# Gated update of a graph network: the new state moves from GpSimd and TensorE transposes to VectorE, and its rows go through DRAM

## Chip, cores and metric

The kernel runs on one core of a Trainium2 chip. The metric is the device time of one execution in microseconds (us); the median of several runs is given where there are several. Everything is computed in float32.

## The reference, cut to what matters

There are 128 graphs of 128 nodes with 256 channels. Layer 0 is a gated update (a GRU cell) over a normalized state `h`; its result is added to `x`. Layer 1 works on the first 25 nodes of each graph only and adds its result to these.

```python
h = jnp.maximum(_layernorm(x, axis=-1), 0.0)
...
xc = jnp.transpose(x, (0, 2, 1))
h = jax.nn.relu(_bn(_conv1d(xc, conv1_w, 0), ...))
h = _bn(_conv1d(h, conv2_w, 8), ...)
x_conv = jnp.transpose(jax.nn.relu(h + xc), (0, 2, 1))
...
x_nmp = jnp.einsum('bnm,bmd->bnd', A, msg)
x_in = jnp.concatenate([x_conv, x_nmp], axis=-1)
gi = x_in @ w_ih.T + b_ih
gh = x @ w_hh.T + b_hh
...
r = jax.nn.sigmoid(gi_r + gh_r)
z = jax.nn.sigmoid(gi_z + gh_z)
nn_ = jnp.tanh(gi_n + r * gh_n)
return (1.0 - z) * nn_ + z * x          # here x is h
...
x = x + _L0_gnn_ref(h, adj, ...)
h = jnp.maximum(_layernorm(x, axis=-1), 0.0)
x = x + _L1_gnn_ref(h, adj, ...)        # changes x[:, :25] only
```

## The kernel before

The work is tiled in 32 groups (`NQ`) of four graphs. It has three stretches. First come the normalization, the first convolution and a Fourier form of the second one (`stage_a`, `stage_b`), in two batches, with the neighbour sums (`early`) beside them; the states `hTd` and the neighbour sums `xmd` are kept in DRAM. Then comes the gated stage (its first new state is computed at 719.7 us), `stage_c(q)`, one group after the other, and beside it layer 1: `rows(q)` normalizes the 32 first rows of the four graphs of a group, `prepare(blk)` builds the adjacency of a block of 16 graphs (4 groups, 8 blocks), `block(blk)` runs its two graph convolutions. At the end stands what is left of layer 1.

The order of the instructions is written by a small planner (`Lane`, `Order`, L156 to L208): each of the functions above is a generator, and `yield a, b` tells the planner that the step took `a` us of TensorE and that its next step is due `b` us later at the earliest. The planner emits the steps of several lanes into one program per engine; each engine runs its own list in order. A `yield` is thus no wait on the chip: the waits come from the data (semaphores that the framework sets), and an instruction whose data is late holds up all that stands behind it on its engine.

In `stage_c` a group works on channels in the partitions and on 512 columns (4 graphs of 128 nodes). The names are `hT` (the state h, tile hTc in the profile, three buffers), `xm` (neighbour sums), `xc` (convolution), `r` (first the reset gate r, then the new state n), `z` (the update gate), `xt` (x, for the sum), each of the last three with one buffer. Products go through `part` (L754) into three PSUM banks named gat and five named tmp. `sums` (L597) makes the differences tc, th and tm on VectorE, tc at the start of a group and th, tm of the next group during it. The last step of a group (L874 to L911) is what is changed:

- ScalarE takes tanh of the two channel halves (L877).
- GpSimd computes, for each half, d = h - n (L880), d = d z (L881) and the new state d + n, written into z in another order of its columns (L883): six operations on 128x512 for each group.
- At least 11 us of planner time later, inside the next group, TensorE turns the result in eight 128x128 transposes (L900) into two tmp banks, so that nodes are in the partitions; VectorE adds x to it, for the first 32 nodes into `X1[blk]`, the tile of layer 1 (L903), for the others into xt (L904, L906).
- GpSimd's queue stores xt to the output in four DMAs (L909), with runs of 1 KB.
- x itself was loaded into xt by SP's queue in four DMAs (L381, called in L831), in rows of 1 KB, in the middle of the group. The tile z of the next group is taken only after these stores have been emitted (L821).

`rows(q)` starts once the group is in `C_DONE`: VectorE's bn_stats on 128x256 of `X1` (L958), aggregation, a power on GpSimd (L961), the scaling on VectorE (L964) and a relu on ScalarE (L965). `prepare` starts with four DMAs of adjacency entries in runs of 100 B (aj, L977), eight small sums on GpSimd (L983) and five reductions on VectorE (L988). `block` stores its rows through GpSimd's queue (L1120).

Of the kernel before, what the change touches and what calls it, by code (L numbers as in the profile page):

```python
# [9 lines left out]
FP = mybir.dt.float32  # L10
# [9 lines left out]
P = 128  # L20
# [187 lines left out]
def kernel(ctx: ExitStack, tc: tile.TileContext, x, adj, consts, vecs, w_se, conv1_w,  # L208
# [14 lines left out]
    wfd = dr.tile([F, D, D], FP, name="wfd")  # L223
    xmd = [dr.tile([P, 2, 512], FP, name=f"xmd{q}") for q in range(NQ)]
    yd = [dr.tile([P, F, D], FP, name=f"yd{b}") for b in range(NBAT)]


    cst = cp.tile([P, CONSTS.shape[1]], FP, name="cst")
# [150 lines left out]
    def load_x(t, q):  # L379
        for j in range(GB):  # L380
            nc.sync.dma_start(out=t[j * WIDE:(j + 1) * WIDE],  # L381
                              in_=x[q * GB + j].rearrange("(t n) c -> n t c", n=WIDE))
# [343 lines left out]
    def stage_c(q):  # L726
# [45 lines left out]


        xs = [(0, hT, None), (2, xm, None), (1, xc, None)]
        r = fr.tile([P, 2, 512], FP, tag="r", name=f"r{q}")
        u2 = fr.tile([P, 2, D], FP, tag="u2", name=f"u2{q}")
        u3 = fr.tile([P, 2, D], FP, tag="u3", name=f"u3{q}")
        r1, r2 = r[:, :, :D], r[:, :, D:]
        early = [(0, hT, th), (2, xm, tm)]
        p1, p6, p5 = bank(wrz, 0), bank(wrz, 5), bank(wrz, 4)  # L780
        part(p1, wrz, 0, xs, True, True)
# [2 lines left out]
        for operation in todo:  # L784
            operation()
        yield 2.6, 0.0
        for ps, i in ((p6, 5), (p5, 4)):
            part(ps, wrz, i, early, True, False)
            yield 1.75, 0.0
# [1 line left out]

        ve = fr.tile([P, 3, 1, D], FP, tag="ve", name=f"ve{q}")
        va, vb, vt = ve[:, 0], ve[:, 1], ve[:, 2]
        r11, r12, r21, r22 = r[:, 0:1, :D], r[:, 0:1, D:], r[:, 1:2, :D], r[:, 1:2, D:]

        def gate(dst, src, row):
            nc.vector.scalar_tensor_tensor(dst, src, v("b_hh", 4 + row), dst,
                                           op0=ALU.add, op1=ALU.mult)
# [4 lines left out]
        h6, h7 = product(wh, 5, xh, ptmp), product(wh, 6, xh, ptmp)  # L803
        nc.vector.tensor_tensor(va, va, h6, ALU.add)
        nc.vector.tensor_tensor(vb, va, h7, ALU.add)
        yield 1.3, 0.0
        part(p1, wrz, 1, xs, False, True, True)
        sigmoid(r1, p1, 0)
# [2 lines left out]
        nc.vector.tensor_tensor(u2, u2, p6, ALU.add)  # L811
        part(h1, wh, 1, xh, False, True, True)
        gate(r11, h1, 0)
        yield 1.3, 0.0
        part(p5, wrz, 4, xs[2:], False, True)
        some_sums(q + 1, 2)
        yield 0.87, 0.0
        if q + 1 in IN:
            convolved(q + 1, IN[q + 1][0])
            yield 1.8, 0.0  # L820
        while q and q - 1 not in C_DONE:  # L821
            yield 0.0, 0.5
        z = fr.tile([P, 2, 512], FP, tag="z", name=f"z{q}")
        z1, z2 = z[:, :, :D], z[:, :, D:]
        nc.vector.tensor_tensor(u3, u2, product(wrz, 6, xs), ALU.add)
        nc.vector.tensor_tensor(z2, u3, p5, ALU.add)
        sigmoid(z2, z2, 2)
        some_sums(q + 1, 2)
        yield 2.6, 0.0
        xt = fr.tile([P, 4, D], FP, tag="xt", name=f"xt{q}")  # L830
        load_x(xt, q)  # L831
        nc.vector.tensor_tensor(z1, u3, product(wrz, 3, xs), ALU.add)
        sigmoid(z1, z1, 2)
        nc.vector.tensor_tensor(vt, vb, product(wh, 3, xh, ptmp), ALU.add)
# [40 lines left out]
        nc.vector.tensor_tensor(r12, r12, p5, ALU.add)  # L875
        for dc in (1, 0):
            nc.scalar.activation(r[:, dc], r[:, dc], AF.Tanh, bias=v("b_ih", 4 + dc))  # L877

            d = hT[:, dc]
            nc.gpsimd.tensor_sub(d, d, r[:, dc])  # L880
            nc.gpsimd.tensor_mul(d, d, z[:, dc])  # L881
            pat = "p (j t n) -> p t j n"
            nc.gpsimd.tensor_add(z[:, dc].rearrange("p (t j n) -> p t j n", t=4, j=GB),  # L883
                                 d.rearrange(pat, j=GB, t=4),
                                 r[:, dc].rearrange(pat, j=GB, t=4))
        G_DONE.add(q)
        yield 0.87, 11.0


        blk = q // QS  # L890
        while blk > 2 and blk - 3 not in F_DONE:
            yield 0.0, 0.5
        if blk not in X1:
            X1[blk] = fr.tile([P, QS, D], FP, tag="x1", name=f"x1_{blk}", bufs=3)
        for h in range(2):
            po = ptmp.tile([P, 2, D], FP, tag="tmp", name=f"po{q}_{h}")
            for i in range(2):
                t = 2 * h + i
                for dc in (1, 0):
                    nc.tensor.transpose(po[:, i, dc * P:(dc + 1) * P],  # L900
                                        z[:, dc, t * P:(t + 1) * P], ident)
            if h == 0:
                nc.vector.tensor_add(X1[blk][:, q % QS], xt[:, 0], po[:, 0])  # L903
                nc.vector.tensor_add(xt[:, 1], xt[:, 1], po[:, 1])  # L904
            else:
                nc.vector.tensor_add(xt[:, 2:], xt[:, 2:], po)  # L906
        yield 0.9, 1.5
        for j in range(GB):
            nc.gpsimd.dma_start(out=out[q * GB + j, WIDE:].rearrange("(t n) c -> n t c", n=WIDE),  # L909
                                in_=xt[j * WIDE:(j + 1) * WIDE, 1:4])  # L910
        C_DONE.add(q)  # L911


# [55 lines left out]
    def prepare(blk):  # L969

        while not (blk - 1 in P_DONE and blk - 2 in {-2, *B1_DONE}):
            yield 0.0, 1.0
        pool, pool2, b1 = S["pool"], S["pool2"], S["b1"]
        ac, r4 = S["ac"][blk % 2], S["r4"][blk % 2]
        aj = pool.tile([NN, SB, NN], FP, tag="dd", name=f"aj{blk}")
        for i in range(GB):
            nc.sync.dma_start(out=aj[:, i % 2 * 2 + i // 2::GB],  # L977
                              in_=adj[blk * SB + i:(blk + 1) * SB:GB, :NN, :NN]
                              .rearrange("b n m -> n b m"))
        yield 0.0, 4.0  # L980

        for r, n, w in _runs():
            nc.gpsimd.tensor_tensor(b1[:, :, r:r + w], aj[:, :, n:n + w],  # L983
                                    ident[:NN, None, n:n + w].to_broadcast([NN, SB, w]),
                                    ALU.add)
        dg = pool2.tile([NN, SB, NG], FP, tag="dg", name=f"dg{blk}")
        for g in range(NG):
            nc.vector.reduce_sum(dg[:, :, g], b1[:, :, OFFS[g]:OFFS[g] + SIZES[g]],  # L988
                                 axis=mybir.AxisListType.X)
        yield 0.0, 7.0  # L990

        pa = ptmp.tile([P, SB // 2, RP], FP, tag="tmp", name=f"pa{blk}")
        for p in range(SB // 2):
            nc.tensor.matmul(pa[:, p], b1[:, 2 * p:2 * p + 2, :].rearrange("n s r -> n (s r)"),
                             c("et")[:NN, :RP], start=True, stop=True)
        nc.vector.tensor_mul(ac, pa, c("same")[:, None, :].to_broadcast([P, SB // 2, RP]))

        pdg = ptmp.tile([P, SB // 2, 2, NG], FP, tag="tmp", name=f"pdg{blk}")
        nc.tensor.matmul(pdg.rearrange("p a s g -> p (a s g)"), c("et")[:NN],
                         dg.rearrange("n b g -> n (b g)"), start=True, stop=True)  # L1000
        dsel = pool.tile([P, SB // 2, 2 * NG], FP, tag="dsel", name=f"dsel{blk}")
        nc.vector.tensor_mul(dsel, pdg.rearrange("p a s g -> p a (s g)"),
                             c("sgrp")[:, None, :].to_broadcast([P, SB // 2, 2 * NG]))
        dm = pool.tile([P, SB // 2], FP, tag="dm", name=f"dm{blk}")
        zo = pool.tile([P, SB // 2], FP, tag="zo", name=f"zo{blk}")
        nc.vector.reduce_sum(dm, dsel, axis=mybir.AxisListType.X)
        nc.vector.tensor_scalar(zo, dm, 0.0, None, op0=ALU.is_equal)
        nc.vector.tensor_add(dm, zo, dm)
        nc.gpsimd.tensor_tensor(dm, dm, c("mhalf"), ALU.pow)
        nc.gpsimd.tensor_mul(zo, zo, dm)  # L1010
        nc.gpsimd.tensor_sub(dm, dm, zo)
        yield 2.0, 7.0

        dd = pool.tile([P, SB // 2, RP], FP, tag="dd", name=f"dd{blk}")
        nc.vector.tensor_mul(dd, c("diag")[:, None, :].to_broadcast([P, SB // 2, RP]),
                             dm[:, :, None].to_broadcast([P, SB // 2, RP]))
        nc.vector.tensor_mul(ac, ac, dm[:, :, None].to_broadcast([P, SB // 2, RP]))
        yield 0.0, 6.0
        pg = ptmp.tile([P, SB // 2, RP], FP, tag="tmp", name=f"pg{blk}")
        nc.tensor.matmul(pg, c("ones2"), dd, start=True, stop=True)  # L1020
        nc.vector.tensor_mul(ac, ac, pg)
        yield 0.9, 3.0

        pr4 = ptmp.tile([P, QS, 2, RP], FP, tag="tmp", name=f"pr4{blk}")
        nc.tensor.matmul(pr4.rearrange("p q a r -> p (q a) r"), c("e4"), ac,
                         start=True, stop=True)
        for j in range(GB):
            s = slice(j * WIDE, (j + 1) * WIDE)
            nc.vector.tensor_copy(r4[s, :, j % 2 * 2 + j // 2, :], pr4[s, :, j % 2, :NR])
        yield 0.9, 1.0  # L1030
        P_DONE.add(blk)
# [112 lines left out]
    for bat, (during_a, during_b) in enumerate(((0.66, 0.5), (0.2, 0.65))):  # L1144
        if bat:
# [13 lines left out]
    groups = Lane([stage_c(q) for q in range(NQ)], ahead=2)  # L1159
    second = [setup_1()] + [part(blk) for blk in range(NBLK) for part in (prepare, block)]  # L1160
    beside.weight = 0.5
    order.run(loads, groups, beside, Lane([rows(q) for q in range(NQ)], ahead=2),
              Lane(second, ahead=2, weight=0.2))


# [39 lines left out]
```

## Time and profile before

| what | value |
|---|---|
| time, median of 3 runs | 2028.95 us (2023.29 to 2034.73) |
| profiled execution, its time | 2029.67 us |
| profiled execution, its span | 2027.9 us |
| mean TensorE clock granted | 0.996 |
| TensorE busy | 1989.1 us, 98% |
| VectorE busy | 1285.4 us, 63% |
| GpSimd busy | 742.3 us, 37% |
| ScalarE busy | 683.7 us, 34% |
| DMA packets | 190266, 281.91 MB |
| GpSimd's short DMA issues of xt (L909) | 128, 569 ns each |

The profile is of one execution. The span goes from the first to the last instruction; the execution's time holds 1.8 us more. PE is TensorE, PEld its weight loads, DVE VectorE, ACT ScalarE, POOL GpSimd and SP the engine that only issues DMAs. A row of a group shows line, engine, operation, tiles (output <- inputs), shapes and count, then busy time and mean duration, then the idle time of the engine just before these instructions and what ended it. The chain that ended last is followed back from the last instruction, at each step to what released it. The issue of a DMA is an instruction on its queue's engine; the duration of the issue is not the time of the transfer.

### The profile page before, as it was taken

The numbers are of one execution on the slowest core, as the hardware profiler recorded it, in microseconds if no ns is written. First come the engines' busy times: TensorE is split into PE (matmuls) and PEld (weight loads), VectorE is DVE, ScalarE is ACT, GpSimd is POOL, SyncE is SP. The second block draws the span as 40 slices with busy tenths as digits, with TensorE's granted clock in tenths as the row PEclk, the third lists the DMA queues.
The fourth block names the chain that finished last, engine by engine and source line by source line (L and its number), as shares of the span: only waits on it lengthen the run. The fifth ranks groups of instructions, "written<-read, shape, count | busy, mean of one in ns | idle before, by whom it ended". The sixth has DMA issues, their size and how long they took to land.

```text
span 2027.9 us, 34053 instructions
## 1 busy us (share of the span) xinstructions
PE 1989.1 (98%) x12852; PEld 1651.6 (81%) x12852; DVE 1285.4 (63%) x2807; ACT 683.7 (34%) x1547; POOL 742.3 (37%) x898
## 2 busy tenths in 40 slices
PE   7998999999999999999999999999999999999998
PEld 5667888889888888878788888878888888878875
DVE  6774445875433566766775775677577757766743
ACT  4663222444222344232322322232233322222233
POOL 3552666333656022622332233224323323332330
PEclk9999999999999999999999999999999999999999
DMA  9997879654887633432322322323232322232122
GB/s 215 296 279 229 275 253 287 209 163 156 265 264 240 191 109 89 149 93 74 95 73 84 104 74 73 104 79 84 79 105 68 90 86 92 81 98 84 37 82 53
DMA packets 190266, 281.91 MB, mean 139 GB/s; under 512 B 23745, under 2 KB 143494, under 8 KB 190102
## 3 DMA queue, kind: packets, MB, share of 16 engines
q1 hardware_dynamic: 157062, 185.46, 31.5%
q0 software_dynamic: 32656, 93.98, 14.2%
q8 instruction: 102, 1.67, 0.4%
q14 instruction: 62, 0.51, 0.1%
q10 hardware_dynamic: 384, 0.28, 0.1%
HBM read 187.34 MB, written 92.27 MB: 138 GB/s over the span
## 4 chain that ended last, share of the span: by engine, by line
PE 91%; DVE 3%; issue 2%; DMA 1%; POOL 1%; ACT 1%; SPq 0%; ACTq 0%; DVEq 0%; POOLq 0%
PE p L754 41%; PE pa L530 7%; PE pm L641 5%; PE ph L1062 5%; PE pz L1071 5%; PE pc L421 5%; PE pb L530 3%; PE pf L432 3%; PE pi L711 3%; PE px L667 3%; PE pw L476 2%; PE ph L410 1%; PE po L900 1%; PE py L1045 1%; PE pse L625 1%
## 5 line engine op out<-in xcount | busy, mean ns | idle before, releaser
L880 POOL TENSOR_TENSOR hTc<-hTc,r 128x512 f32<-128x512 f32 x64 | 88.5, 1383 | 255.5 <-ACT r L877 255.4
L530 PE MATMUL pa<-wf,X 128*128 128x256 f32 x640 | 152.2, 381 | 0.0
L562 DVE SCALAR_TENSOR_TENSOR y<-pa,kk 128x512 f32<-128x512 f32 x78 | 53.8, 690 | 151.3 <-ACT kk L561 151.3
L909 POOL DMA_DIRECT2D out<-xt x128 | 72.0, 569 | 175.3 <-DVE xt L906 172.2
L754 PE MATMUL p<-th,wrz 128*128 128x256 f32 x512 | 134.5, 385 | 0.0
L754 PE MATMUL p<-tc,wrz 128*128 128x256 f32 x512 | 131.5, 379 | 0.0
L754 PE MATMUL p<-tm,wrz 128*128 128x256 f32 x512 | 131.4, 379 | 0.0
L530 PEld LDWEIGHTS pa<-wf,X 128*128 128x128 f32 x640 | 118.1, 190 | 16.2 <-issue 2.0
L641 PE MATMUL pm<-wmsg,hT 128*128 128x256 f32 x512 | 123.6, 387 | 2.2 <-DMA wmsg<-in_w_msg 2.2
L421 PE MATMUL pc<-c1w,hTa 128*128 128x256 f32 x512 | 121.7, 384 | 1.2 <-ACT hTa L412 1.2
L641 PEld LDWEIGHTS pm<-wmsg,hT 128*128 128x128 f32 x512 | 97.0, 193 | 18.4 <-ACT ef L629 2.6
L1064 ACT ACTIVATE hh<-ph,vec 128x96 f32<-128x96 f32 (+3 forms) x160 | 63.8, 401 | 140.7 <-PE ph L1062 131.6
L1062 PE MATMUL ph<-yz,w 128*128 128x96 f32 (+3 forms) x640 | 109.7, 325 | 1.0 <-issue 1.0
L754 PEld LDWEIGHTS p<-th,wrz 128*128 128x128 f32 x512 | 94.6, 190 | 19.2 <-issue 7.4
L421 PEld LDWEIGHTS pc<-c1w,hTa 128*128 128x128 f32 x512 | 94.4, 191 | 18.4 <-DVE h L424 4.8
L723 ACT ACTIVATE xc<-xc,t_bn 128x256 f32<-128x256 f32 x128 | 58.0, 500 | 149.1 <-DVE xc L720 149.1
L754 PEld LDWEIGHTS p<-tm,wrz 128*128 128x128 f32 x512 | 97.3, 190 | 13.2
L1071 PE MATMUL pz<-hh,w 128*128 128x96 f32 (+3 forms) x640 | 107.3, 321 | 0.0
L1062 PEld LDWEIGHTS ph<-yz,w 128*128 128x128 f32 x640 | 88.2, 193 | 21.3 <-issue 15.2
L754 PEld LDWEIGHTS p<-tc,wrz 128*128 128x128 f32 x512 | 94.9, 190 | 11.7
L1071 PEld LDWEIGHTS pz<-hh,w 128*128 128x128 f32 x640 | 86.6, 191 | 17.7
L754 PE MATMUL p<-hTc,wrz 128*128 128x256 f32 x384 | 98.9, 380 | 0.0
(200 smaller groups left out, 4580.1 us busy)
## 6 DMA issues: line engine op xcount, KB each, us to landing
wf<-wfd SPq DMA_DIRECT2D x160, 256.0 KB
wfd<-ws POOLq DMA_DIRECT2D x64, 320.0 KB, 9.5
yd<-y POOLq DMA_DIRECT2D x80, 256.0 KB, 4.2
yt<-yd SPq DMA_DIRECT2D x64, 320.0 KB
w<-in_W SPq DMA_DIRECT2D x40, 512.0 KB
xa<-in_x SPq DMA_DIRECT2D x128, 128.0 KB
hTd<-hTa POOLq DMA_DIRECT2D x32, 512.0 KB, 6.9
hT<-hTd SPq DMA_DIRECT2D x32, 512.0 KB
```

Of the source, the lines that this page charges most:

```text
L421: nc.tensor.matmul(pc[:, i], hT[:, k, (2 * h + i) * N:(2 * h + i + 1) * N], c1w[:, k], start=(k == 0), stop=(k == 1))
L432: nc.tensor.matmul(pf[:, i, :F * NB], h1[:, 2 * h + i, k * P:(k + 1) * P], fwd, start=True, stop=True)
L530: nc.tensor.matmul(ps, xk(k), WF[f][:, k, s], start=(k == 0), stop=(k == 1))
L641: nc.tensor.matmul(pm[:, i], hT[:, k, j * N:(j + 1) * N], LATE["wmsg"][:, k], start=(k == 0), stop=(k == 1))
L667: nc.tensor.matmul(px[:, dc, i], msgs[h][:, i, dc * P:(dc + 1) * P], aT[:, 2 * h + i], start=True, stop=True)
L711: nc.tensor.matmul(pi[w * WIDE:(w + 1) * WIDE, :, :, n].rearrange("p k g c -> p g k c"), inv[:F, o:o + WIDE], yt[:, n // 2::2].rearrange(" ...
L754: nc.tensor.matmul(ps[:, m], w[:, i, k, m * P:(m + 1) * P], factor(i, x, t), start=first and j == 0, stop=last and j == len(n) - 1, skip_g ...
L880: nc.gpsimd.tensor_sub(d, d, r[:, dc])
L909: nc.gpsimd.dma_start(out=out[q * GB + j, WIDE:].rearrange("(t n) c -> n t c", n=WIDE), in_=xt[j * WIDE:(j + 1) * WIDE, 1:4])
L1062: nc.tensor.matmul(ph, w1[:, k, m * P:(m + 1) * P], yz[:, k, :, o:o + n], start=(k == 0), stop=(k == 1))
L1064: nc.scalar.activation(hh[:, m], ph, AF.Relu, bias=v("b1", g * 4 + m))
L1071: nc.tensor.matmul(pz, w2[:, g, m, cc * P:(cc + 1) * P], hs[g][:, m], start=(m == 0), stop=(m == 3))
```

## The change

The new state is computed by VectorE instead of GpSimd, for one channel half at a time, at two places in the following group (`turned`): three 128x512 operations and one VectorE transpose, which turns blocks of 32x32 and writes into the group's hT. A third place (`returned`) adds the x of the group in one operation on 128x1024 and stores the sum to a new DRAM tensor `x1d[q]` in four DMAs of GpSimd's queue. The 32x32 blocks leave the result in an order in which 32 neighbouring channels of a node are together: xt has this order too, x is loaded into it in four DMAs of GpSimd's queue, and both the load and the store move runs of 32 floats (128 B), 1024 of them in each DMA. A new generator `fetch(q)`, in a lane of its own, is due 10 us of planner time after `returned`: it loads the first 32 nodes of the four graphs from `x1d[q]` to `X1` and copies the other 96 from DRAM to the output, both through GpSimd's queue; 9 us later the group counts as done for `rows`. TensorE's eight transposes, their PSUM banks, and the wait of the planner for the group before (L821) are gone. The tile r of a group is now taken after the second `turned`. For the last group the three steps follow one another at once. In `prepare` the small sums of GpSimd are due 13 us after their loads instead of 4, and the reductions 5 us after the sums.

```diff
@@ -223,6 +223,7 @@
     wfd = dr.tile([F, D, D], FP, name="wfd")
     xmd = [dr.tile([P, 2, 512], FP, name=f"xmd{q}") for q in range(NQ)]
     yd = [dr.tile([P, F, D], FP, name=f"yd{b}") for b in range(NBAT)]
+    x1d = [dr.tile([GB, N, D], FP, name=f"x1d{q}") for q in range(NQ)]
 
 
     cst = cp.tile([P, CONSTS.shape[1]], FP, name="cst")
@@ -772,10 +773,8 @@
 
 
         xs = [(0, hT, None), (2, xm, None), (1, xc, None)]
-        r = fr.tile([P, 2, 512], FP, tag="r", name=f"r{q}")
         u2 = fr.tile([P, 2, D], FP, tag="u2", name=f"u2{q}")
         u3 = fr.tile([P, 2, D], FP, tag="u3", name=f"u3{q}")
-        r1, r2 = r[:, :, :D], r[:, :, D:]
         early = [(0, hT, th), (2, xm, tm)]
         p1, p6, p5 = bank(wrz, 0), bank(wrz, 5), bank(wrz, 4)
         part(p1, wrz, 0, xs, True, True)
@@ -784,6 +783,7 @@
         for operation in todo:
             operation()
         yield 2.6, 0.0
+        turned(q - 1, 1)
         for ps, i in ((p6, 5), (p5, 4)):
             part(ps, wrz, i, early, True, False)
             yield 1.75, 0.0
@@ -791,7 +791,6 @@
 
         ve = fr.tile([P, 3, 1, D], FP, tag="ve", name=f"ve{q}")
         va, vb, vt = ve[:, 0], ve[:, 1], ve[:, 2]
-        r11, r12, r21, r22 = r[:, 0:1, :D], r[:, 0:1, D:], r[:, 1:2, :D], r[:, 1:2, D:]
 
         def gate(dst, src, row):
             nc.vector.scalar_tensor_tensor(dst, src, v("b_hh", 4 + row), dst,
@@ -803,6 +802,10 @@
         h6, h7 = product(wh, 5, xh, ptmp), product(wh, 6, xh, ptmp)
         nc.vector.tensor_tensor(va, va, h6, ALU.add)
         nc.vector.tensor_tensor(vb, va, h7, ALU.add)
+        turned(q - 1, 0)
+        r = fr.tile([P, 2, 512], FP, tag="r", name=f"r{q}")
+        r1, r2 = r[:, :, :D], r[:, :, D:]
+        r11, r12, r21, r22 = r[:, 0:1, :D], r[:, 0:1, D:], r[:, 1:2, :D], r[:, 1:2, D:]
         yield 1.3, 0.0
         part(p1, wrz, 1, xs, False, True, True)
         sigmoid(r1, p1, 0)
@@ -811,6 +814,7 @@
         nc.vector.tensor_tensor(u2, u2, p6, ALU.add)
         part(h1, wh, 1, xh, False, True, True)
         gate(r11, h1, 0)
+        returned(q - 1)
         yield 1.3, 0.0
         part(p5, wrz, 4, xs[2:], False, True)
         some_sums(q + 1, 2)
@@ -818,17 +822,18 @@
         if q + 1 in IN:
             convolved(q + 1, IN[q + 1][0])
             yield 1.8, 0.0
-        while q and q - 1 not in C_DONE:
-            yield 0.0, 0.5
         z = fr.tile([P, 2, 512], FP, tag="z", name=f"z{q}")
+        xt = fr.tile([P, 16, 2, WIDE], FP, tag="xt", name=f"xt{q}")
         z1, z2 = z[:, :, :D], z[:, :, D:]
         nc.vector.tensor_tensor(u3, u2, product(wrz, 6, xs), ALU.add)
         nc.vector.tensor_tensor(z2, u3, p5, ALU.add)
         sigmoid(z2, z2, 2)
         some_sums(q + 1, 2)
         yield 2.6, 0.0
-        xt = fr.tile([P, 4, D], FP, tag="xt", name=f"xt{q}")
-        load_x(xt, q)
+        TURN[q] = xt, hT, z, r
+        for a in range(4):
+            nc.gpsimd.dma_start(out=xt[a * WIDE:(a + 1) * WIDE].rearrange("p b d c -> p (b d) c"),
+                                in_=slices(x[q * GB:(q + 1) * GB])[a])
         nc.vector.tensor_tensor(z1, u3, product(wrz, 3, xs), ALU.add)
         sigmoid(z1, z1, 2)
         nc.vector.tensor_tensor(vt, vb, product(wh, 3, xh, ptmp), ALU.add)
@@ -875,39 +880,55 @@
         nc.vector.tensor_tensor(r12, r12, p5, ALU.add)
         for dc in (1, 0):
             nc.scalar.activation(r[:, dc], r[:, dc], AF.Tanh, bias=v("b_ih", 4 + dc))
-
-            d = hT[:, dc]
-            nc.gpsimd.tensor_sub(d, d, r[:, dc])
-            nc.gpsimd.tensor_mul(d, d, z[:, dc])
-            pat = "p (j t n) -> p t j n"
-            nc.gpsimd.tensor_add(z[:, dc].rearrange("p (t j n) -> p t j n", t=4, j=GB),
-                                 d.rearrange(pat, j=GB, t=4),
-                                 r[:, dc].rearrange(pat, j=GB, t=4))
         G_DONE.add(q)
-        yield 0.87, 11.0
-
-
+        yield 0.87, 0.0
+        if q == NQ - 1:
+            yield 0.0, 1.0
+            turned(q, 1)
+            turned(q, 0)
+            returned(q)
+
+    def slices(t):
+        return t.rearrange("j n c -> (j n c)").rearrange(
+            "(s k a c) -> a s k c", s=WIDE, k=2 * 16, a=4)
+
+    TURN, T_DONE = {}, set()
+
+    def turned(q, dc):
+
+        if q in TURN:
+            _, hT, z, r = TURN[q]
+            d, zd = hT[:, dc], z[:, dc]
+            nc.vector.tensor_sub(d, d, r[:, dc])
+            nc.vector.tensor_mul(d, d, zd)
+            nc.vector.tensor_add(zd, d, r[:, dc])
+            nc.vector.transpose(d.rearrange("p (b c) -> p b c", c=WIDE),
+                                zd.rearrange("p (s b) -> p b s", b=16))
+
+    def returned(q):
+
+        if q in TURN:
+            xt, hT, _, _ = TURN.pop(q)
+            nc.vector.tensor_add(xt, xt, hT.rearrange("p d (b c) -> p b d c", c=WIDE))
+            for a in range(4):
+                nc.gpsimd.dma_start(
+                    out=slices(x1d[q])[a],
+                    in_=xt[a * WIDE:(a + 1) * WIDE].rearrange("p b d c -> p (b d) c"))
+            T_DONE.add(q)
+
+    def fetch(q):
+
+        while q not in T_DONE:
+            yield 0.0, 0.5
+        yield 0.0, 10.0 if q < NQ - 1 else 6.0
         blk = q // QS
         while blk > 2 and blk - 3 not in F_DONE:
             yield 0.0, 0.5
         if blk not in X1:
-            X1[blk] = fr.tile([P, QS, D], FP, tag="x1", name=f"x1_{blk}", bufs=3)
-        for h in range(2):
-            po = ptmp.tile([P, 2, D], FP, tag="tmp", name=f"po{q}_{h}")
-            for i in range(2):
-                t = 2 * h + i
-                for dc in (1, 0):
-                    nc.tensor.transpose(po[:, i, dc * P:(dc + 1) * P],
-                                        z[:, dc, t * P:(t + 1) * P], ident)
-            if h == 0:
-                nc.vector.tensor_add(X1[blk][:, q % QS], xt[:, 0], po[:, 0])
-                nc.vector.tensor_add(xt[:, 1], xt[:, 1], po[:, 1])
-            else:
-                nc.vector.tensor_add(xt[:, 2:], xt[:, 2:], po)
-        yield 0.9, 1.5
-        for j in range(GB):
-            nc.gpsimd.dma_start(out=out[q * GB + j, WIDE:].rearrange("(t n) c -> n t c", n=WIDE),
-                                in_=xt[j * WIDE:(j + 1) * WIDE, 1:4])
+            X1[blk] = LATE["co"].tile([P, QS, D], FP, tag="x1", name=f"x1_{blk}", bufs=3)
+        nc.gpsimd.dma_start(out=X1[blk][:, q % QS], in_=x1d[q][:, :WIDE])
+        nc.gpsimd.dma_start(out=out[q * GB:(q + 1) * GB, WIDE:], in_=x1d[q][:, WIDE:])
+        yield 0.0, 9.0 if q < NQ - 1 else 4.0
         C_DONE.add(q)
 
 
@@ -977,12 +998,14 @@
             nc.sync.dma_start(out=aj[:, i % 2 * 2 + i // 2::GB],
                               in_=adj[blk * SB + i:(blk + 1) * SB:GB, :NN, :NN]
                               .rearrange("b n m -> n b m"))
-        yield 0.0, 4.0
+        yield 0.0, 13.0 if blk < NBLK - 1 else 6.0
 
         for r, n, w in _runs():
             nc.gpsimd.tensor_tensor(b1[:, :, r:r + w], aj[:, :, n:n + w],
                                     ident[:NN, None, n:n + w].to_broadcast([NN, SB, w]),
                                     ALU.add)
+        yield 0.0, 5.0
+
         dg = pool2.tile([NN, SB, NG], FP, tag="dg", name=f"dg{blk}")
         for g in range(NG):
             nc.vector.reduce_sum(dg[:, :, g], b1[:, :, OFFS[g]:OFFS[g] + SIZES[g]],
@@ -1159,7 +1182,8 @@
     groups = Lane([stage_c(q) for q in range(NQ)], ahead=2)
     second = [setup_1()] + [part(blk) for blk in range(NBLK) for part in (prepare, block)]
     beside.weight = 0.5
-    order.run(loads, groups, beside, Lane([rows(q) for q in range(NQ)], ahead=2),
+    order.run(loads, groups, beside, Lane([fetch(q) for q in range(NQ)], ahead=2),
+              Lane([rows(q) for q in range(NQ)], ahead=2),
               Lane(second, ahead=2, weight=0.2))
 
 
```

## The prediction

> **What bounds the kernel now.** I read the page's first and fourth part (who is busy, which chain ended last), then the table of windows over the gated stage, where all of the change lies, then the tile of the removed transposes, the VectorE and GpSimd groups, and the DMA answers for narrow windows.
>
> ```profile
> PE 1989.1 (98%) x12852; PEld 1651.6 (81%) x12852; DVE 1285.4 (63%) x2807; ACT 683.7 (34%) x1547; POOL 742.3 (37%) x898
> ...
> PE 91%; DVE 3%; issue 2%; DMA 1%; POOL 1%; ACT 1%; SPq 0%; ACTq 0%; DVEq 0%; POOLq 0%
> ```
> ```profile
> core 0: us, PE busy (x) PEld busy (x) DVE busy (x) ACT busy (x) POOL busy (x), PEclk, DMA share, GB/s
> 1290.00:1943.00 653.00, 653.00 (x4218) 545.57 (x4218) 451.07 (x944) 190.07 (x413) 210.85 (x234) 1.00 0.27 81
> ```
> TensorE holds 91% of the chain. The window 1290 to 1943 us holds the last 17 groups, 38.4 us each: TensorE 653 of 653 us, VectorE 451 (69%), GpSimd 211 (32%), DMA 0.27, full clock. So here a TensorE instruction that goes is worth its whole time, as long as VectorE, GpSimd or a transfer does not become late.
>
> ```profile
> L900 PEld LDWEIGHTS po<-cst,z x256: 138/141/150, 733.5 to 1954.5; 128*128 128x128 f32 x128
> L900 PE MATMUL po<-cst,z x256: 270/273/330, 733.7 to 1954.7; 128*128 128x128 f32 x128
> ```
> ```profile
> 1920.63 0.87 PE po L900 x8
> ...
> 1954.06 0.87 PE po L900 x8
> ```
> The tile's answer counts 256 transposes, 8 for each of the 32 groups. Their 273 ns overlap; the chain in order of time gives what 8 of them take from the engine, 0.87 us.
>
> [...]
> ```profile
> L597 DVE TENSOR_TENSOR tc<-xc 128x256 f32<-128x256 f32 x64 | 77.5, 1211 | 0.2 <-ACT xc L723 0.2
> L597 DVE TENSOR_TENSOR tc<-tc,xc 128x256 f32<-128x256 f32 x32 | 46.4, 1450 | 0.0
> L597 DVE TENSOR_TENSOR tc<-xc,tc 128x256 f32<-128x256 f32 x32 | 43.2, 1351 | 1.2
> L597 DVE TENSOR_TENSOR th<-hTc 128x256 f32<-128x256 f32 x64 | 26.7, 418 | 0.0
> L880 POOL TENSOR_TENSOR hTc<-hTc,r 128x512 f32<-128x512 f32 x64 | 88.5, 1383 | 255.5 <-ACT r L877 255.4
> ```
> The same subtraction takes 418 ns alone and 1211 to 1450 ns at the start of a group, just where L880 to L883 run. [...] No small write to HBM is in this trace. [...] In the trace 512 KB from L687 lands in 5.8 us, 96 KB from L909 in 3.7.
>
> **TensorE.** 256 transposes go: 256 x 0.87/8 = 27.8 us. Nothing is added.
>
> **VectorE.**
> ```profile
> L718 DVE STREAM_TRANSPOSE xc<-pi 128x512 f32<-128x512 f32 x64 | 45.6, 713 | 2.8 <-PE pi L711 0.8
> L865 DVE TENSOR_TENSOR r<-r,v 128x512 f32<-128x512 f32 x32 | 22.2, 694 | 1.1
> L906 DVE TENSOR_TENSOR xt<-xt,po 128x512 f32<-128x512 f32 x32 | 21.7, 680 | 0.0
> ```
> A half is three 128x512 operations at 694 and a transpose at 713 ns: 2.8 us. (The transpose reads with a stride; L438, a strided copy of 320 elements, takes 483 ns, on the line between 256 and 512, so I add nothing; if reads doubled, 0.7 us a half.) The 1024-element sum: 256 elements take 421 ns (L866), 512 take 694, so 694 + 2x273 = 1.24 us. Added per group 2x2.8 + 1.24 = 6.8 us; removed L903, L904, L906: 1.5; recovered, as GpSimd's six operations go, 2x1.211+1.45+1.351 - 4x0.42 = 3.5. Net +1.8 us: VectorE from 26.5 of 38.4 us to 28.3 of 37.5, 75%. As to place: the first half follows the four tc operations; these shrink by 3.5 us and L804 waits another 1.5 us on average, together more than 2.8. The second half stands ahead of L811, which waits for TensorE 2.9 us on average (80 us, 29 times). The sum takes the place of the three additions. Behind them in VectorE's queue stand the first sigmoid of the new r (ACT may not overwrite r before it is read) and L811; TensorE needs their banks a product later. I take nothing, and up to 0.7 us a group (22 us) as the upper end.
>
> **GpSimd's queue.** Out go six operations (8.0 us a group) and four stores at 569 ns. In come four stores and four loads with 1024 runs each, one fetch, one copy to the output. 1024 runs are not in the trace: L909 has 96 and takes 569 ns, L687 has 128 and takes 552, L456 has 256 and takes 611. From the last two, 0.46 ns a run, 0.96 us for 1024; from below 0.57; proportional to L909, 6.1 us. I take 0.6 to 1.0: some 8 us a group with the fetch, less than the 10.3 that go. The loads wait there for the stores to land; behind them stand the fetch, the rs power and prepare's sums, none of which TensorE needs sooner than a block later.
>
> **SP's queue** loses four loads a group and its wait for out<-xt (152 us in all); hTc stood behind it and comes earlier, which nothing waits for.
>
> **DMA.** The window 1391.2 to 1391.7 us holds only runs of 100 B (the aj load):
> ```profile
> DMA packets 155, 0.01 MB, mean 29 GB/s; under 512 B 155, under 2 KB 155, under 8 KB 155
> ## 3 DMA queue, kind: packets, MB, share of 16 engines
> q1 hardware_dynamic: 155, 0.01, 30.1%
> ```
> 0.301 x 16 x 0.5 us / 155 = 15.5 ns a run, for a read. The write of 128 B is unknown: from below the same 15.5, from above a whole kilobyte's price (L909's 3 KB rows, 187 ns each in the window 1312 to 1319, give 62). I take 31[...]. Per group and engine: 256x15.5 + 256x31 = 11.9 us in, about 2 out (512 KB in 1 KB packets at 61 ns); share 0.27 to about 0.54, 0.75 at 62 ns. Bandwidth is no bound.
>
> **The chain that is new.** The rows go out to DRAM and come back before bn_stats (L958 before) may read them. From the end of the 1.24 us sum: issue 0.6, drain 256w (4096 runs over 16 engines, w for one write), [...]load issue 0.6, loads' drain 4.0 ahead of the fetch in the same queue, the fetch 0.5[...] 9.7 + 256w, which is 17.6 us at w = 31 ns. The planner puts bn_stats at least 10 + 9 = 19 us behind; in the built program a median of 33.5 VectorE instructions of some 56 a group lie between, 22 us of 37.5. So it arrives in time, by 1 to 4 us. If it is late, VectorE stands, and behind it the gate sums that free TensorE's banks.
>
> **The end.** After group 31's last product (1942.9) the last rows are needed at 1986.7: 44 us of block 6 cover two tanh 1.5, two halves and the sum 6.8, store and fetch about 16, rows 5: 29. Nothing.
>
> **Sum.** Profiled execution 2029.67 (span 2027.9) - 27.8 = 2001.9. The median of the runs is 2028.95, 0.7 lower: 2001.
>
> **Rivals.** *A, as summed*, 0.62: 1993 to 2012 (gaps ahead of the weight loads that waited for L904, 8 us in all, may go too). *B, VectorE late*: the halves do not fit their gaps, 0.7 us a group, 2001 + 22 = 2023; for it, they sit inside the gate chain; against, the gaps above. 0.13. *C, slower: the fetched rows come late to bn_stats.* It decides from 9.7 + 256w over 20.5 us (the deadline and 1.5 us that the banks give), w over 42 ns. At 62 ns the chain is 25.6, 5 us late, for the 24 groups whose rows are read inside the stage: 2121; half-way, 3 us, 2073. For it, nothing shows such writes; against, the 22 us. 0.20. *D, GpSimd bound by its runs*: at 6.1 us an issue, 8 take 49 us of a 37.5 us group, with the rest some 14 us over, 32 times: 2450. Against it, 256 runs cost no more than 128. 0.05.
>
> **How the numbers follow.** A measurement tells about 0.5% from no change, 10 us: 2019 and 2039. Faster: A and the better part of B, 0.66; same: the rest of B, 0.09; slower: C and D, 0.25. The range runs from A's lower end to the near part of C: 1993 to 2060.
>
> **What would show it.** No po in TensorE's groups and TensorE still full in the stage; tc operations near 420 ns; in the waits, L811 no longer waiting on TensorE but nothing on TensorE's side waiting on VectorE; the short-run issues under 1.1 us; bn_stats with little wait for a DMA. I am wrong if bn_stats waits microseconds a group for x1d, if the short stores take more than 42 ns a run, if an issue takes several us, or if weight loads wait for r.

## The result and the profile after

The changed kernel takes **2018.37 us** (median of 19 runs, 2012.23 to 2026.85), the kernel before 2028.95 (19 runs, 2021.83 to 2037.08). The ratio is 0.9949, 95% interval 0.9936 to 0.9963: it is faster, by 10.6 us where the prediction had 28. The profiled execution of after took 2023.75 us (span 2022.0) at a mean granted clock of 0.991; that of before 2029.67 at 0.996.

The page of after, busy time and chain by engine:

```profile
PE 1968.3 (97%) x12596; PEld 1630.7 (81%) x12596; DVE 1351.0 (67%) x2999; ACT 683.4 (34%) x1547; POOL 657.6 (33%) x898
...
PE 88%; DVE 6%; DMA 3%; issue 1%; ACT 1%; SPq 1%; POOL 0%; DVEq 0%; ACTq 0%; POOLq 0%
```

TensorE has 256 instructions less and lost 20.8 us of busy time, not 27.8. VectorE gained 65.6 us, and its share of the chain went from 3% to 6%: for a while it is VectorE that sets the time. The table of windows for the last 17 groups shows that it is not there:

```profile
core 0: us, PE busy (x) PEld busy (x) DVE busy (x) ACT busy (x) POOL busy (x), PEclk, DMA share, GB/s
1290.00:1920.00 630.00, 629.12 (x4011) 525.95 (x4010) 476.77 (x1023) 184.47 (x402) 162.87 (x231) 0.99 0.38 101
```

In these groups TensorE is still full, VectorE at 76%, DMA at 0.38; only the clock is 0.99 instead of 1.00. The VectorE and GpSimd groups show the prices:

```profile
L905 DVE STREAM_TRANSPOSE hTc<-z 128x512 f32<-128x512 f32 x64 | 67.3, 1051 | 2.2
L903 DVE TENSOR_TENSOR hTc<-hTc,z 128x512 f32<-128x512 f32 x64 | 44.3, 692 | 2.2
L912 DVE TENSOR_TENSOR xt<-xt,hTc 128x1024 f32<-128x1024 f32 x32 | 38.9, 1216 | 0.2 <-DVE r L796 0.2
L598 DVE TENSOR_TENSOR tc<-xc 128x256 f32<-128x256 f32 x64 | 27.0, 422 | 0.2 <-ACT xc L724 0.2
L979 DVE BATCH_NORM_STATS2 st<-x 128x6 f32<-128x256 f32 x32 | 13.5, 421 | 6.8 <-DMA x<-x1d 6.8
```
```profile
L914 POOL DMA_DIRECT2D x1d<-xt x128 | 101.1, 815 | 462.8 <-DVE xt L912 450.5 <-DVE yz L1070 12.3
L835 POOL DMA_DIRECT2D xt<-in_x x128 | 100.2, 789 | 181.0 <-DMA x1d<-xt 173.7 <-issue 6.6
```

The operations, the issues with 1024 runs (815 and 789 ns) and the tc operations came as priced: tc takes 418 to 445 ns by form here, where before had 1211 to 1450. Of before's 128 tc operations 122 ran beside GpSimd's six operations of a group; the other six took 418 to 425 ns. Only the turn costs 1051 ns instead of 713. The fetched rows are late to L979 by 6.8 us in all, in three places, 5.7 of it once, behind the last group.

The view that shows most is TensorE's timeline around the end of the last group. The columns are start, duration, engine, line, operation and tiles; in brackets the idle time ahead and what ended it:

```profile
1922.05 0.66 PE L1128 MATMUL pg<-zt,ac 64*64 64x256 f32 x8
1930.59 1.78 PE L1068 MATMUL py<-r,x1h 128*128 128x212 f32 x4 [7.87 <-DVE zt L1131]
1932.30 1.12 PE L1138 MATMUL pfu<-zt,s2w 128*64 128x256 f32 x4
1933.35 1.78 PE L1068 MATMUL py<-r,x1h 128*128 128x212 f32 x4
...
1937.56 0.98 PE L1068 MATMUL py<-r,x1h 128*128 128x212 f32 x4
1939.06 1.25 PE L1085 MATMUL ph<-yz,w 128*128 128x400 f32 x3 [0.52 <-issue]
```

TensorE stands for 7.87 us, and then its first matmuls take 1.78 instead of 0.98 us: half the clock. What VectorE did meanwhile:

```profile
1921.23 0.76 DVE L1131 TENSOR_TENSOR zt<-pg,b2row 128x256 f32<-128x256 f32 x2 [0.25 <-ACT r L882]
...
1922.64 0.68 DVE L902 TENSOR_TENSOR hTc<-hTc,r 128x512 f32<-128x512 f32 x1
...
1925.76 0.65 DVE L902 TENSOR_TENSOR hTc<-hTc,r 128x512 f32<-128x512 f32 x1
...
1927.90 1.04 DVE L905 STREAM_TRANSPOSE hTc<-z 128x512 f32<-128x512 f32 x1
1928.97 1.22 DVE L912 TENSOR_TENSOR xt<-xt,hTc 128x1024 f32<-128x1024 f32 x1
1930.11 0.75 DVE L1131 TENSOR_TENSOR zt<-pg,b2row 128x256 f32<-128x256 f32 x2
```

The last group's two halves and its sum (1922.64 to 1930.19) stand in VectorE's queue between two of block 5's sums zt (L1131). These free the banks that py and pg are waiting for. Nobody needs the last rows for another 40 us; block 5 needs its sums at once.

A second difference is in the clock. In the stage the trace has short intervals, 3.4 us each, in which the granted clock is half; each makes the work 1.7 us longer. Before had two between the first gate matmul and block 6, after has five, besides the 10.2 us at half clock that begin in the wait above. Four of after's five, and both of before's, begin 0.5 to 1.6 us behind the degree matmuls pa, which read 25 of 128 rows. Of after, windows of TensorE around one of them (window, length, busy time, clock, DMA share, GB/s), and its timeline there:

```profile
core 0: us, PE busy (x), PEclk, DMA share, GB/s
1500.00:1506.00 6.00, 6.00 (x45) 0.99 0.46 91
1506.00:1509.40 3.40, 3.40 (x17) 0.52 0.41 148
```
```profile
1502.68 1.99 PE L1017 MATMUL pa<-cst,b 25*128 25x64 f32 x16
1504.51 0.40 PE L1022 MATMUL pdg<-dg,cst 25*128 25x80 f32 x2
...
1505.80 3.50 PE L1094 MATMUL pz<-hh,w 128*128 128x96 f32 x16
```

TensorE was busy for all of it, so no idle time explains this one. All half-clock intervals of before and of after start whole multiples of 3.413 us apart: in after, from 785.65 to 877.81 us it is 27 times that, to 935.84 another 17, to 1505.87 another 167. The 10.2 us of the wait begin on the same grid, at 1925.70 us, when TensorE has stood for 3.0 of the 7.87 us.

### The profile page after: what moved, and what is told of

Its sections match the earlier page's. It is cut to its first block, busy times and chain, and to the rows that moved or that the text cites. A ratio compares the mean times of both kernels' runs of the same rounds, so it can differ in the third digit from the quotient of the medians.

```text
span 2022.0 us, 33340 instructions
## 1 busy us (share of the span) xinstructions
PE 1968.3 (97%) x12596; PEld 1630.7 (81%) x12596; DVE 1351.0 (67%) x2999; ACT 683.4 (34%) x1547; POOL 657.6 (33%) x898
## 4 chain that ended last, share of the span: by engine, by line
PE 88%; DVE 6%; DMA 3%; issue 1%; ACT 1%; SPq 1%; POOL 0%; DVEq 0%; ACTq 0%; POOLq 0%
PE p L755 41%; PE pa L531 7%; PE pz L1094 5%; PE ph L1085 5%; PE pm L642 5%; PE pc L422 4%; PE pb L531 3%; PE pf L433 3%; PE px L668 3%; PE pi L712 3%; DMA xa<-in_x 1%; PE py L1068 1%; PE pw L477 1%; PE ph L411 1%; PE pfu L1138 1%
## 5 line engine op out<-in xcount | busy, mean ns | idle before, releaser
L914 POOL DMA_DIRECT2D x1d<-xt x128 | 101.1, 815 | 462.8 <-DVE xt L912 450.5
L835 POOL DMA_DIRECT2D xt<-in_x x128 | 100.2, 789 | 181.0 <-DMA x1d<-xt 173.7
L1094 PEld LDWEIGHTS pz<-hh,w 128*128 128x128 f32 x640 | 89.1, 197 | 18.7 <-DVE yz L1096 1.3
## 6 DMA issues: line engine op xcount, KB each, us to landing
wfd<-ws POOLq DMA_DIRECT2D x64, 320.0 KB, 10.2
```

What stands on the lines that cost most here:

```text
L835: nc.gpsimd.dma_start(out=xt[a * WIDE:(a + 1) * WIDE].rearrange("p b d c -> p (b d) c"), in_=slices(x[q * GB:(q + 1) * GB])[a])
L914: nc.gpsimd.dma_start(out=slices(x1d[q])[a], in_=xt[a * WIDE:(a + 1) * WIDE].rearrange("p b d c -> p (b d) c"))
L1094: nc.tensor.matmul(pz, w2[:, g, m, cc * P:(cc + 1) * P], hs[g][:, m], start=(m == 0), stop=(m == 3))
```

## The experiments

**Theory 1**: the end took the missing time, by the order in VectorE's queue and not by VectorE's load. **Theory 2**: the half-clock intervals behind pa took it. **Theory 3**: the transposes were never worth 28 us.

The part ahead of the first gate matmul is the same in all kernels, yet it ends between 675.2 and 690.8 us in these profiles. So besides the medians I compare two parts of the profiled execution: from the first gate matmul to the first ph of block 6 ("stage"), and from there to the end ("tail").

### Moving the last group's steps, first try

```diff
         if q == NQ - 1:
-            yield 0.0, 1.0
+            yield 0.0, 6.0
             turned(q, 1)
```

> The last group's two halves and its sum into xt are put later in VectorE's order: behind the sums zt of block 5 and two of its pfu sums, instead of ahead of the zt sums. Theory 1 (what stands behind these steps in VectorE's queue set the end back): TensorE's wait of 7.9 us for zt goes, and with it the stretch of half clock that followed (2.6 us); 8 to 10.5 us less than the changed kernel, 2008 to 2010 us. Theory 2 (the loss lies in intervals of half clock after thin matmuls in the stage): the wait moves or shrinks, the time changes by less than 3 us. Theory 3 (the transposes were never worth 28 us): no change, since nothing was lost at the end.

Measured: 2016.84 us, ratio to before 0.995 (0.9934 to 0.9965); no gain over the changed kernel. The waits of TensorE behind 1880 us, in us in total, times and longest:

```profile
PE ph L1085 <- ACT yz L1071: 6.5, 1, 6.5
...
PE py L1068 <- DVE zt L1131: 0.4, 1, 0.4
```

The wait for zt is gone, 7.9 to 0.4, but 6.5 us of it came back a little further on: the steps now stood between the copies of py (L1070) that ph waits for. The expectation missed; the place still has to be right.

### The steps in three pieces

```diff
             turned(q, 1)
+            yield 0.0, 1.5
             turned(q, 0)
+            yield 0.0, 1.5
             returned(q)
```

> The last group's two halves and its sum are kept where they begin, but other work may come between them (1.5 us of the schedule between each). Theory 1: the single wait of 7.9 us becomes two or three of 1 to 3 us, and the clock stays full; 4 to 9 us less than the changed kernel, 2009 to 2014 us. Theory 2: within 3 us of the changed kernel. Theory 3: no change.

Measured: 2014.09 us, 0.9931 (0.9914 to 0.9949), 4.3 us below the changed kernel, though the intervals overlap. The longest wait is one of 3.5 us for zt. The gain fits the weak end of theory 1, but the clock did not stay full: the window 1920.35 to 1927.20 us, behind this wait, has a clock of 0.51.

### Full rows for pa

```diff
-        S["b1"] = pool.tile([NN, SB, RP], FP, name="b1")
+        S["b1"] = pool.tile([P, SB, RP], FP, name="b1")
...
-                             c("et")[:NN, :RP], start=True, stop=True)
+                             c("et")[:, :RP], start=True, stop=True)
```

The other readers and writers of b1 take its first 25 rows; the added rows are zero.

> The changed kernel with the degree matmuls (pa) of the preparing step read over all 128 rows, the added rows zero, instead of 25; the same number of matmuls and columns. Theory 2 (the intervals of half clock follow these thin matmuls): the four intervals in the stage at 878, 936, 1506 and 1663 us go, each worth about 1.7 us, so 4 to 7 us less (2011 to 2014), and the granted clock rises by 0.003 to 0.005. Theory 1: the end and its wait of 7.9 us stay. If the intervals come from something else, the time stays within 2 us and they stay, at other places.

Measured: 2016.35 us, 0.9941 (0.9923 to 0.996). The five intervals in the stage are gone from the profile and the clock is 0.995, but the median fell by 2 us only, less than the interval can tell. The wait of 7.9 us is unchanged. The same edit on the kernel before:

> The kernel before with the degree matmuls (pa) over all 128 rows, as in the padded changed kernel. Theory 2: its two intervals of half clock in the stage (1015 and 1636 us) go, 3 to 4 us less than the kernel before, 2025; against it the padded changed kernel (2016.4) is then 9 us faster, so most of the missing 17 us is not a matter of these intervals. If the padded matmuls only cost or gain something of their own, no change.

Measured: 2024.38 us against 2031.12 for before in the same set, 0.9972 (0.9962 to 0.9983). Both intervals behind pa are gone; one at 840 us is new, behind waits of 1.5 and 0.8 us. So the cause of the intervals behind pa is right: in the stage, six profiled kernels without the padding had 2 to 5 intervals, 15 of the 18 behind pa; ten with it had 0 or 1, none behind pa. But the padding gains at least as much for before as for after (the mean clock of all runs rises by 0.002 in both). **Theory 2 falls** as the reason for the shortfall. Its use is another: with padded kernels on both sides the difference can be read without these intervals.

### The bare worth of the transposes

Before, without the 256 transposes; the sums take z as it lies:

```diff
-            po = ptmp.tile([P, 2, D], FP, tag="tmp", name=f"po{q}_{h}")
...
-                    nc.tensor.transpose(po[:, i, dc * P:(dc + 1) * P],
-                                        z[:, dc, t * P:(t + 1) * P], ident)
+            po = z[:, :, h * D:(h + 1) * D]
```

> The kernel before without the 256 transposes po (left out: the turning of the new state; the sums take the state unturned from SBUF), all else as before, so it shows the bare worth of the transposes. If they were worth what their busy time says, 25 to 28 us less than the kernel before, 2001 to 2004 us. Theory 3 (they hid a wait that stays): at most 15 us less, 2014 us or more.

Measured: 2007.13 us, 0.9894 (0.987 to 0.9917), 21 us. This lies between the two expectations and decides nothing; the profile has three intervals behind pa, before has two. And padded:

> The padded kernel before without the 256 transposes po (left out: the turning of the new state). Without the intervals after pa the bare worth of the transposes should come out as their busy time: 25 to 28 us less than the padded kernel before, 1998 to 2000 us. Theory 3: 22 us or less, as the unpadded pair showed (2007.1 against 2028.5).

Measured: 1999.39 us, 0.9858 (0.9836 to 0.9879), 25.0 us below the padded before. TensorE by windows, stage and tail, first of the padded before and then of this kernel (columns: window, length, busy time of TensorE and its instructions, granted clock, DMA share, GB/s):

```profile
679.23:1941.89 1262.66, 1255.37 (x8196) 1.00 0.30 88
1941.89:2023.30 81.41, 73.59 (x494) 0.97 0.27 74
```
```profile
675.22:1911.40 1236.18, 1227.39 (x7949) 1.00 0.30 90
1911.40:1993.10 81.70, 72.58 (x486) 0.96 0.27 73
```

The busy time of the stage falls by 28.0, of which 1.7 is the one interval at half clock; TensorE's idle time rises by 1.5 (7.29 to 8.79). So the transposes are worth about 25 us, and **theory 3 falls**, but for 2 to 3 us.

### No steps, and late steps, for the last group

```diff
         if q == NQ - 1:
             yield 0.0, 1.0
-            turned(q, 1)
-            turned(q, 0)
-            returned(q)
+            returned(q, False)
```

> The padded changed kernel without the last group's two halves and sum on VectorE (left out: update, turning and sum of the last four graphs, whose x is stored as it came). Theory 1: the wait of 7.9 us for zt and the 10 us of half clock behind it go, 9 to 10.5 us less than the padded changed kernel (2016.4), 2006 to 2007. Theory 2 alone: less than 3 us.

Measured: 2003.64 us, 0.9887 (0.9867 to 0.9907), 12.7 us below the padded changed kernel (2016.35, in another set of runs, at 0.9941), more than the 9 to 10.5 expected. Then the complete kernel with `yield 0.0, 12.0` in that place, which puts the steps behind all four copies of py:

> The padded changed kernel, complete, with the last group's two halves and sum put behind block 5's sums and block 6's four copies of py in VectorE's order, where TensorE has 7.6 us of ph without VectorE. Theory 1: no wait for zt or py copies is left; 8 to 10 us less than the padded changed kernel, 2006 to 2008.5, if the last rows, which come 9 us later, are still in time for block 7 at about 1970 us; a wait of py for x1h of up to 5 us there if not.

Measured: 2004.73 us, 0.9879 (0.986 to 0.9899), 11.6 us below. Stage and tail, first of the padded changed kernel, then of the late one:

```profile
682.46:1931.67 1249.21, 1230.08 (x7948) 1.00 0.39 106
1931.67:2014.50 82.83, 72.08 (x486) 0.98 0.25 74
```
```profile
683.84:1922.85 1239.01, 1227.28 (x7948) 1.00 0.39 106
1922.85:2005.10 82.25, 72.08 (x486) 0.98 0.29 81
```

The whole difference lies in the stage's end: 7.4 us of idle time (19.13 to 11.73) and 2.8 of busy time at half clock. The tail is no longer than in the padded changed kernel, so the last rows are still in time, though their steps begin 8.5 us behind the start of the last group's tanh instead of 2.2. **Theory 1 holds**: the gain is 11.6 us by the medians, which come from two sets of runs, and 10.8 by the profiles, where 8 to 10 were expected. Without the padding:

> The changed kernel, unpadded, with only the last group's two halves and sum put behind block 6's copies of py in VectorE's order. Theory 1: the same 10 to 12 us less than the changed kernel as in the padded pair (2016.35 to 2004.7), 2006 to 2009, about 20 us less than the kernel before. Theory 2: the intervals of half clock in the stage come back and cost 2 to 4 us against the padded one, 2007 to 2009.

Measured: 2009.2 us, 0.9908 (0.9883 to 0.9933); three intervals at half clock in its stage. Late and padded together is the best complete version here, 26 us below the 2031.12 of before in its set.

### Work in the wait

To part the wait from the clock, 28 matmuls that nobody reads, in TensorE's order just ahead of the waiting py:

```diff
+            if blk == NBLK - 2 and q == 0:
+                fill = pgat.tile([P, 2, D], FP, tag="gat", name="fill")
+                for i in range(28):
+                    nc.tensor.matmul(fill[:, i % 2], ident, b2row, start=True, stop=True)
```

> The padded changed kernel with 28 matmuls more (identity by a row of constants, 128x256, some 6.1 us, read by nothing) in TensorE's order where it waits 7.9 us for zt. If the half clock behind the wait (10.2 us of it) comes from the standstill, it goes, py takes 0.98 us again instead of 1.78, and the time falls by about 2.5 us to 2014. If the clock falls for another reason, no change. Theory 1 asks that the rest of the wait stays, so no fall by more than 4 us.

Measured: 2014.59 us, 0.9926 (0.9908 to 0.9944). The timeline of TensorE:

```profile
1911.85 12.35 PE L1070 MATMUL fill<-b2row,cst 128*128 128x256 f32 x56
1924.04 0.88 PE L1072 MATMUL py<-r,x1h 128*128 128x212 f32 x4
```

The fill took 12.35 us, not 6.1 (each of these float32 matmuls counts as two records). It is 4.5 us longer than the wait it covers. Still, from the start of the last pg to the first ph it is 18.7 us here and 17.4 in the padded changed kernel, 1.3 more instead of 4.5: py runs at full clock, and no half clock follows. So the standstill does bring the half clock, at about 3 us. The medians (2014.59 and 2016.35) cannot show this: their intervals overlap.

### The last 3 us: three tries

The late kernel's stage is still idle for 11.7 us, the bare removal's for 8.8. TensorE's waits for r, the last sums of a group, are 5.7 us in 7 places in every changed kernel, 2.0 in 4 in the padded kernel before. First guess, the preparing step's waiting times:

```diff
-        yield 0.0, 13.0 if blk < NBLK - 1 else 6.0
+        yield 0.0, 4.0
...
-        yield 0.0, 5.0
```

> The padded kernel with the late last group, and the preparing step's waiting times as in the kernel before (one of 4.0 instead of 13.0 and 5.0). The changed kernels wait 5.7 us in 7 places for the sums r at the end of a group, the kernels before 2.0 us in 4; in two of these places steps of the preparing step (dd and ac) stand ahead of r. If the new waiting times moved them there, those waits fall to 2 to 3 us and the time by 2 to 4 us, 2001 to 2003. If VectorE's added work of 65 us is what makes r late, no change.

> The padded kernel before with only the preparing step's waiting times of the changed kernel (13.0 and 5.0 instead of 4.0). If these move the steps ahead of r, waits for r rise to about 5 us and the time by 2 to 4 us, 2026 to 2028; if not, within 1 us of the padded kernel before (2024.4).

Measured: 2009.43 us, 0.9898 (0.9876 to 0.992), waits for r still 5.7 in 7; and 2023.76 us, 0.9972 (0.9963 to 0.9982), waits for r 3.6 in 5, the time as the padded before. Wrong guess for the late kernel; in the kernel before, the waits for r rose from 2.0 to 3.6 us, without a loss of time. Second, VectorE's load: the three operations of the update given to GpSimd as before (in the first), or left out (in the second).

```diff
             nc.scalar.activation(r[:, dc], r[:, dc], AF.Tanh, bias=v("b_ih", 4 + dc))
+            d = hT[:, dc]
+            nc.gpsimd.tensor_sub(d, d, r[:, dc])
+            nc.gpsimd.tensor_mul(d, d, z[:, dc])
+            nc.gpsimd.tensor_add(z[:, dc], d, r[:, dc])
...
-            nc.vector.tensor_sub(d, d, r[:, dc])
-            nc.vector.tensor_mul(d, d, zd)
-            nc.vector.tensor_add(zd, d, r[:, dc])
```

> The padded late kernel with the update (sub, mul, add on 128x512, 192 instructions) back on GpSimd behind tanh, as before; VectorE keeps the turning and the sum. So it is the change without the part that moves the update. If VectorE's 133 us of update are what makes r late, the waits for r fall from 5.7 to 2 to 3 us and the time by 2 to 3 us from 2004.7, unless the differences tc beside GpSimd (1.2 to 1.45 us each before, 0.42 after) come back and take it, then no change or 1 us more.

> The padded late kernel without the update (left out: the three operations that make the new state; the gate z is turned and summed in its place), on no engine. If VectorE's added work makes r late, TensorE's time not busy falls to about 8.8 us and the whole to 2001 to 2002; if the new order does, no change from 2004.7.

Measured: 2010.47 us, 0.9913 (0.9891 to 0.9935), and 1999.99 us, 0.9857 (0.9834 to 0.9879). The waits for r are 5.7 us in 7 places in both, as in the line of the kernel without the update:

```profile
PE p L755 <- DVE r L875: 5.7, 7, 1.8
PE pz L1091 <- DVE yz L1093: 0.7, 1, 0.7
```

So these waits do not come from VectorE's load by the update. What is left is the other moved steps, the turn and the sum among them, by their place or their load; these were not parted. The update has a price of its own: without it most other waits go and the stage's idle time falls from 11.73 to 7.65. On GpSimd it saves nothing. Up to the start of the last group's tanh that kernel needs as long as the late one, 1230.3 us each; then one new wait comes:

```profile
1917.97 10.43 PE L1086 MATMUL ph<-yz,w 128*128 128x400 f32 x32 [3.16 <-ACT yz L1072]
```

The last update takes 7.9 us there (1907.49 to 1915.38), and the rows' factor rs stands behind it in GpSimd's queue. VectorE waits 4.56 us for rs, ahead of three of its copies of py, TensorE stands 3.16 instead of 0.52 us, and ph takes 10.43 instead of 7.62 us: 5.4 of the 5.7 us. It is the fault of the changed kernel again, in another queue.

## Why the prediction was wrong

| part of the sum, us | predicted | measured |
|---|---|---|
| busy time of the transposes | -27.8 | -26.4 in the stage (1255.37 to 1227.28 is 28.1, less 1.7 at half clock); its 8 in the tail are in the last row |
| stage, TensorE waiting, mostly for VectorE | 0 | +4.4 (7.29 to 11.73 idle, late kernel) |
| end, waiting | 0 | +7.4 (11.73 to 19.13 idle) |
| end, half clock | 0 | +2.8 |
| tail (81.41 to 82.83) | in the first row | +1.4, its own transposes' 0.9 included |
| sum | -27.8 | -10.4 |

The last column is from the padded profiles, whose stage and tail differ by 12.0 us; the 1.7 us of the one interval at half clock in the padded before are taken out. The medians say 10.6 without the padding and 8.0 with it. In the tail one wait is new, of py for r (L1052), 1.1 us; the rest of its growth was not traced.

- **TensorE**: right. The work went, 26.4 us of it in the stage, where the estimate gives 27.0 for 248 transposes; the bare removal is worth 25.0.
- **The end, "Nothing"**: this step failed, and it alone took 10 to 12 of the 17.4 us that are missing. It asked only when the last rows are needed (44 us later, which held: the late kernel begins the steps 6.3 us later, with no loss). It did not ask what stands behind the steps on VectorE: eight operations and the sum, 7.5 us, ahead of block 5's sums, for which TensorE waits at once. In the other 31 groups the gate work is interleaved with the steps by hand; in the last group nothing parts them, and the update had run on GpSimd, where block 5 did not notice it.
- **Full clock**: an unspoken assumption. A wait of 7.9 us is dearer than 7.9, by 2.8.
- **VectorE, "nothing, up to 0.7 us a group"**: nearly right. The stage lost 2.9 us more than the bare removal (11.73 against 8.79), 0.1 us a group. TensorE's waits for r, which it should not have had more of, went from 2.0 to 5.7 us. The turn was mis-sized, 1051 against 713 ns; the gaps took it.
- **GpSimd, DMA, the fetch chain**: right in the outcome. Issues take 0.8 us, and the rows are late by more than 0.2 us in two groups only. The load on the DMA was put too high, 0.54 against 0.38. The chain from the sum to the landing of the rows came out, 14.5 to 20.7 us with a median of 17.6 where 17.6 was foreseen, in part by luck: the stores landed 9.2 us behind the sum instead of 10.5, and from there the rows took 8.2 instead of 7.1. No trace had shown the 4.0 us for the two landings in its 9.7, and 31 ns a write was an estimate, twice the 15.5 of a read. Rivals C and D did not come. B's time, 2023, is near the result, but its mechanism, halves that do not fit their gaps, is not what the runs show.

Open: which of the moved steps makes r late in 7 places, and what the rest of the tail's growth is.

## What to carry to other kernels

When work moves to another engine's in-order queue, ask two things of its last instance too: when its result is needed, and who stands behind it in that queue. The second is easily missed where a loop ends, as the steps that were interleaved there now come in one piece. A planner with a delay for such a step can put it under work that leaves the engine alone, here 7.6 us of ph; check what it lands ahead of, since a step put off by too little only meets the next waiting instruction.

## What the runs showed of the hardware

- Matmuls over 25 of 128 rows (pa and the two pdg behind it, 2.2 us in sequence, with TensorE busy) can be followed by 3.4 us at half clock. Whether they are goes with their place on the grid of 3.413 us on which the half-clock intervals start. The six profiled kernels without padding have 48 such sequences: all 15 that lie wholly within one step of the grid are followed by half clock, and one of the 33 that reach over two steps (in before and after five of five, and one of eleven). With pa over 128 rows, zeros in the added ones, none of the 20 that lie within one step is followed by it, in ten kernels, and one of the other 60, which has a wait of 0.82 us ahead of it.
- Short waits of TensorE went with half clock too: it began behind a single wait of 1.95 us (at 1057.9 us, the padded late kernel with other preparing times) and within one of 3.16 us (at 1916.9 us, the kernel with the update on GpSimd), behind which ph took 10.43 us; behind 0.52 us it took 7.62.
- In after, a stream transpose of 128x512 float32 takes 1051 ns where it reads SBUF with a stride of 16 elements (L905), 709 where it reads PSUM in order (L719). Stride and memory differ at once here, so no run parts them.
- A store or load of 1024 runs of 128 B takes GpSimd 0.79 to 0.82 us to issue (L835 and L914 of after), one of 256 runs 0.61 (L456 of before), one of 128 runs 0.55 (L687 of before).
